# The opening normalisation of a chunk in a Mamba stage: one body earlier, its variance copied out of PSUM, its last product and x3's sum in other slots

## The chip, the cores and the metric

The kernel runs on one core of one Trainium2 chip. The metric is device time in microseconds (us). The engines are called PE (TensorE; PEld is its weight load), DVE (VectorE), ACT (ScalarE), POOL (GpSimd) and SP (SyncE, which here only issues DMAs). "Lnnn" is a line of the kernel before.

## The reference, cut to what matters

Two "metaformer" layers follow one another. The change lies in the token mixer of the second, a stack of eight Mamba layers on 4 images of 4096 tokens with 128 channels:

```python
x = x + _L1_conv_ref(_ln_c(x), ...)          # second layer's mixer
...
def _ln_c(v, eps=1e-6):
    m = jnp.mean(v, axis=1, keepdims=True)
    s = jnp.var(v, axis=1, keepdims=True)
    return (v - m) / jnp.sqrt(s + eps)
...
for l in range(DEPTH):                       # DEPTH = 8
    seq = _mamba_layer(seq, W_in[l], ...)    # conv, gates, a scan over time with 16 states per channel
    seq = _rmsnorm(seq, rms_w[l])
```

`_ln_c` is a normalisation over the 128 channels of each token: mean, difference, variance, reciprocal root, product. It stands once, ahead of the first Mamba layer. The sum `x + ...` stands once, behind the eighth.

## The kernel before, in words

Channels lie on the 128 partitions. `mamba` cuts the 4096 tokens into 8 chunks of 512. Its unit of work is a **body**: one chunk, one layer, one image. There are 8 x 8 x 4 = 256 bodies, numbered chunk x 32 + layer x 4 + image, so bodies 32k to 32k+3 are a chunk's first layer and 32k+28 to 32k+31 its eighth. Each body has 16 **slots** (j = 0 to 15). In a slot the loop at L1181 emits, in this order: two exponentials dA for the slot after next (`decay`, ACT, L973); 16 small matmuls dBx for the next slot (`inputs`, PE, L995), into one of two PSUM buffers; perhaps one step of the *previous* layer's recurrence (`rec.step`: matmul L669 on PE, tanh L672 on ACT), which runs interleaved with this stage; two scans of the slot (DVE, L1028), which need dA and dBx; behind each odd slot one product of four states with C (`times_c`, POOL, L1041 copy and L1044 product, called c0 to c7 here); then the "side" work of the slot; and 8 transposing matmuls that add up a slot's result four slots later (`add_up`, PE, L1048; in slots 0 to 3 they belong to the body before).

The side work is written out by hand in the table PLAN (L692): a row for each slot, and a bar that parts what stands ahead of `add_up` from what stands behind it. A letter names the body that a piece works for, seen from the current body o = i: n = i+1, q = i-1, m = i+2. In the kernel before, s is body i+2 and z body i+3, each only where that body belongs to layer 0. Every engine runs its instructions in the order emitted. The pieces that matter here:

- `v0`, `v1` (L846): the input projection of the next body, in PSUM banks f0 and f1, with the ACT work behind it (L849 to L855).
- `s.mean` (L808): one matmul with the averaging matrix into bank f1 (L810, two passes in the trace), the difference on DVE (L812), its square on ACT (L813). `s.var` (L815): a second matmul into bank f1 (L818) and, directly from the bank, the logarithm on ACT (L819). `s.rstd` (L1105): the exponential on ACT. `s.u` (L1109): the product on POOL. `z.fetch` (L806): the load of the next such body's input, into a single buffer.
- `q.pm`, `q.log`, `q.rstd`, `q.u` (L1098, L1102, L1105, L1109): the same kind of step for the RMS norm that ends a body.
- `q.end` (L1111): for layer 8 alone, a load of 256 KB, the sum on POOL (L1115), a store.
- `dtx1`, `turn1` (L934 on POOL, L941 on PE, L944 on ACT): the second half of the next body's scan inputs: a POOL product, four transposes into bank f1, a copy.
- `m.edge` (L822): eight small POOL instructions (L829, L835, L836).

Banks f0 and f1 are handed round among these pieces by the table BANK (L712), so that each piece waits until the reader of the one before it is done.

Bodies in which layer 0 is normalised or layer 8 is summed lie around each of the seven chunk borders. In the kernel before, s is active in bodies 30 to 33 (mod 32) and `q.end` in bodies 29 to 32. Ahead of the loop, bodies 0 and 1 are normalised in a straight line (L1157).

Of the kernel before, what the change touches and what calls it, by code (L numbers as in the profile page):

```python
# [8 lines left out]
F32 = mybir.dt.float32  # L9
AF = mybir.ActivationFunctionType  # L10
ALU = mybir.AluOpType
# [8 lines left out]
P = 128  # L20
B = 4
# [24 lines left out]
TL = 512  # L46
# [643 lines left out]


PLAN = """  # L692
n.v0 |
s.mean |
| n.tap03 n.tap02 o.C3
n.v1 | q.leave1 o.by0
n.tap01 | o.by1 q.back1
q.gate1 |
| n.tap12 q.po0 n.tap13 n.tap11
q.po1 | q.square n.pz0 n.pz1 n.silu n.silu_z0 n.silu_z1 a.exp  # L700
n.pd0 | n.pd1 n.keep
n.pt0 n.C2 n.pt1 | n.softplus0 q.pm n.softplus1 a.ln q.log q.rstd s.var s.rstd a.exp
n.dtx0 n.bt n.B |
q.u s.u | o.leave0 n.diag0
q.end n.turn0 n.skip0 n.skip1 | n.diag2
o.back0 n.diag5 | n.diag3
n.diag1 z.fetch n.C0 o.gate0 n.dtx1 m.edge | n.C1
n.diag4 n.turn1 n.diag6 |
""".strip().split("\n")
STEPS = [1, 0, 1, 2, 1, 1, 1, 0, 1, 0, 1, 0, 2, 2, 2, 1]  # L710

# [15 lines left out]
def mamba(tc, ops, I, rec, x2_d, x3_d):  # L727
# [8 lines left out]
    nc = tc.nc  # L736
# [5 lines left out]
    with ExitStack() as ctx:  # L742
# [4 lines left out]
        w = ctx.enter_context(tc.tile_pool(name="mwk", bufs=2))  # L747
        c = ctx.enter_context(tc.tile_pool(name="mc", bufs=1))
        wp = ctx.enter_context(tc.tile_pool(name="mwp", bufs=2))
        up = ctx.enter_context(tc.tile_pool(name="mu", bufs=5))  # L750
        w1 = ctx.enter_context(tc.tile_pool(name="mw1", bufs=1))
        dr = ctx.enter_context(tc.tile_pool(name="mdr", bufs=4, space=DRAM))
        psf = ctx.enter_context(tc.tile_pool(name="mpf", bufs=1, space=PSUM))
# [27 lines left out]
        us = {}  # L781
        weights = {}

        def bank(what):

            name = f"f{BANK[what]}"
            return psf.tile([P, TL], F32, tag=name, name=name)
# [10 lines left out]
        def load(l):  # L798
            given = wp.tile([P, W_GIVEN], F32, tag="given", name="given")
            nc.sync.dma_start(out=given, in_=I["m_given"][l])  # L800
            weights[l] = given


        def fetch(o):
            o.x2 = w1.tile([P, TL], F32, tag="x2", name="x2")
            nc.sync.dma_start(out=o.x2, in_=x2_d[:, o.b, o.ck * TL : (o.ck + 1) * TL])  # L806
# [8 lines left out]
        def var(o):  # L815
            o.r = w1.tile([P, TL], F32, tag="r0", name="r0")
            v = bank("var")
            nc.tensor.matmul(v, ops.avg, o.x2, start=True, stop=True)  # L818
            nc.scalar.activation(o.r, v, AF.Ln, bias=ops.eps6)  # L819


        def edge(o):  # L822

            o.edge = w.tile([P, NH, DC - 1], F32, tag="edge", name="edge")
            part = w.tile([P, NH, DC - 1, DC - 1], F32, tag="part", name="part")
            for h in range(NH):
                tl = tail[:, o.l, o.b, h, :]
                for k in range(DC - 1):
                    nc.gpsimd.tensor_tensor(  # L829
                        part[:, h, k, :],  # L830
                        tl[:, k : k + DC - 1],
                        taps[:, o.l, h, k : k + 1].to_broadcast([P, DC - 1]),
                        ALU.mult,
                    )
            nc.gpsimd.tensor_tensor(o.edge, part[:, :, 0, :], part[:, :, 1, :], ALU.add)  # L835
            nc.gpsimd.tensor_tensor(o.edge, o.edge, part[:, :, 2, :], ALU.add)  # L836
# [140 lines left out]
        def decay(o, j):  # L977
            if where(j)[0] != SP_B:
                o.dA[j] = dap.tile([P, 2, TL], F32, tag="dA", name="dA")
                exps(o, j)  # L980

        def inputs(o, j):


            sp, h = where(j)
            if sp == SP_B:
                o.dA[j] = psx.tile([P, 2, TL], F32, tag="dBx", name="dAp")
                exps(o, j)
                return
            o.dBx[j] = psx.tile([P, TL, 2], F32, tag="dBx", name="dBx")  # L990
            for n in range(NB):
                for q in range(2):
                    at = q * HQ + n * 64
                    row = slice(q * 64, (q + 1) * 64)
                    nc.tensor.matmul(  # L995
                        o.dBx[j][:, at : at + 64, :],
                        o.dtxT[h][row, n, :],
                        o.diag[row, sp, n],
                        start=True,
                        stop=True,  # L1000
                    )
# [21 lines left out]
        def scan(o, j):  # L1023
            sp, h = where(j)
            hs = states(o, j)
            for k in range(2):
                s = 2 * sp + k
                nc.vector.tensor_tensor_scan(  # L1028
                    hs[:, k, :],
                    o.dA[j][:, k, :],  # L1030
                    hs[:, k, :] if sp == SP_B else o.dBx[j][:, :, k],
                    state[:, o.l, o.b, h, s : s + 1],
                    ALU.mult,
                    ALU.add,
                )

        def times_c(o, g):
            sp, h = where(2 * g)
            f = sp // 2
            hs = o.hs[g]  # L1040
            nc.gpsimd.tensor_copy(  # L1041
                state[:, o.l, o.b, h, 4 * f : 4 * f + 4].unsqueeze(2), hs[:, :, TL - 1 : TL]
            )
            nc.gpsimd.tensor_tensor(hs, hs, o.Cb[f], ALU.mult)  # L1044
# [13 lines left out]
        def skips(o, h):  # L1058

            o.yT = psy.tile([P, NB, P], F32, tag="yT", name="yT")  # L1060
            add_turned(o, o.xD[h], start=True)

        def add_up(o, j):
            for k in range(2):
                add_turned(o, states(o, j)[:, k, :])
# [39 lines left out]
            nc.scalar.activation(o.r, o.r, AF.Exp, scale=-0.5)  # L1105

        def norm(o):
            us[o.b] = up.tile([P, TL], F32, tag="u", name="u")
            nc.gpsimd.tensor_tensor(us[o.b], o.pos, o.r, ALU.mult)  # L1109

        def end(o):  # L1111
            here = (slice(None), o.b, slice(o.ck * TL, (o.ck + 1) * TL))
            x3 = w1.tile([P, TL], F32, tag="x3", name="x3")
            nc.sync.dma_start(out=x3, in_=x2_d[here])
            nc.gpsimd.tensor_tensor(x3, x3, us[o.b], ALU.add)  # L1115
            nc.sync.dma_start(out=x3_d[here], in_=x3)


# [1 line left out]
        bodies = [Body(ck, l, b) for ck in range(NCK) for l in range(DEPTH) for b in range(B)]  # L1120

        def get(i):
            return bodies[i] if 0 <= i < len(bodies) else None

        def table(name):
# [12 lines left out]
        pieces |= {f"by{h}": lambda o, h=h: times_b(o, SP - 1 + h) for h in range(NH)}  # L1138
        pieces |= {f"C{g}": lambda o, g=g: give_c(o, g) for g in range(NS // 4)}
        pieces |= {  # L1140
            "fetch": fetch, "mean": mean, "var": var, "silu": silu_x, "keep": keep, "B": give_b,
            "bt": turn_b, "square": square, "pm": rms, "log": log, "rstd": rstd, "u": norm,
            "end": lambda o: end(o) if o.l == DEPTH - 1 else None, "edge": edge,
            "exp": table(EXP_TANH), "ln": table(EXP_LN),
        }
        plan = [[[x.split(".") for x in part.split()] for part in row.split("|")] for row in PLAN]

        def side(who, j, part):

            for k, what in plan[j][part] if part < len(plan[j]) else ():  # L1150
                if who.get(k):
                    pieces[what](who[k])

        load(0)
        for t in range(PRE):
            rec.step(t)
        for s in bodies[0:2]:  # L1157
            for what in ("fetch", "mean", "var", "rstd", "u"):
                pieces[what](s)
        fetch(bodies[2])  # L1160
        edge(bodies[0])
        for row in plan:
            for part in row:
# [7 lines left out]
        LAG = 4  # L1171
        t = PRE
        for i in range(len(bodies) + 1):
            o, n, q, s = get(i), get(i + 1), get(i - 1), get(i + 2)
            who = {"o": o, "n": n, "q": q, "m": s, "a": o or q}
            z = get(i + 3)
            who["s"] = s if s and s.l == 0 else None
            who["z"] = z if z and z.l == 0 else None
            if o and o.b == 1 and i + 3 < len(bodies):
                load((o.l + 1) % DEPTH)  # L1180
            for j in range(NSLOT):  # L1181
                if o:
                    if j + 2 < NSLOT:
                        decay(o, j + 2)
                    elif n:
                        decay(n, j + 2 - NSLOT)
                    if j + 1 < NSLOT:
                        inputs(o, j + 1)
                    elif n:
                        inputs(n, 0)  # L1190
                    if STEPS[j] > 0 and t < L:
                        rec.step(t)
                        t += 1
                    scan(o, j)
                    if j % 2:
                        times_c(o, j // 2)
                side(who, j, 0)
                if o and j in (LAG, SP + LAG):
                    skips(o, j // SP)
                if o and j >= LAG:  # L1200
                    add_up(o, j - LAG)
                elif q and j < LAG:
                    add_up(q, NSLOT - LAG + j)
                side(who, j, 1)
                if o and STEPS[j] > 1 and t < L:
                    rec.step(t)
                    t += 1
# [424 lines left out]
```

## Time and profile before

| | us |
|---|---|
| time, median of 3 runs | 15802.7 (15797.8 to 15809.1) |
| the profiled execution's own time | 15798.8 |
| its span | 15796.6 |
| first and last scan of the Mamba stage | 2209.0 and 15491.5 |

The Mamba stage is 13,282 us of the span. Distance from a body's first scan to that of the next, from the start times of L1028 in the timeline of DVE:

| body (border between chunks 1 and 2) | 61 | 62 | 63 | 64 | 65 | 66 | 67 | 68 |
|---|---|---|---|---|---|---|---|---|
| us | 50.78 | 57.66 | 58.35 | 59.05 | 60.98 | 53.54 | 50.80 | 51.51 |

Away from the borders a body takes 50.78 us, and 51.5 us where its number is divisible by 4 (a new tile of the interleaved recurrence begins there). The windows view from body 0's first scan to 3743 us and from 4034 to 5359 us has PEclk, the granted TensorE clock, at 1.00; from 3743 to 4034 us and from 5359 to 5700 us, the five bodies at a border, it is 0.96.

How to read the views: the timeline lists an engine's instructions by start, with merged length, and in brackets the idle time ahead of them and what ended it; the windows view has one row for each stretch, with busy time by engine and the granted clock. A group's row on the page has count, then busy time and mean duration, then idle time ahead of it.

### The profile page before, as it was taken

What the parts mean: (1) busy time and instruction counts of PE and PEld (TensorE: products, weight loads), DVE (VectorE), ACT (ScalarE), POOL (GpSimd) and SP (SyncE); (2) the same over time, 40 slices, a digit from 0 to 9 for tenths busy, and PEclk for the clock granted to TensorE, in tenths of its full rate; (3) what the DMA queues carried; (4) which work ended last, traced back from release to release, by engine and by line L of the source; (5) the groups of instructions that cost most, each with busy time, mean ns of one, the idle gap of its engine ahead of it and who ended that gap; (6) DMA issues with size and microseconds to landing.
All of it is one profiled execution on the core that took longest, in us unless ns stands there. A gap on an engine that the chain in (4) does not pass through costs nothing. (4 is left out here: it accounts for less than half of the span.)

```text
span 15796.6 us, 303059 instructions
## 1 busy us (share of the span) xinstructions
PE 14414.7 (91%) x120596; PEld 10829.8 (69%) x120596; DVE 13673.8 (87%) x14937; ACT 12011.2 (76%) x23557; POOL 13179.6 (83%) x9086
## 2 busy tenths in 40 slices
PE   7888779999999999999999999999999999989996
PEld 3444557777777777777777777777777777766664
DVE  8998039998999889998999899989998999989994
ACT  6887248887888778877888788878887788777773
POOL 4555039998999999998999899989999999999993
PEclk8999579999999999999999999999999999999998
DMA  0000012222222222222222222222222222222224
GB/s 22 22 22 22 15 55 98 100 104 99 101 97 99 106 96 103 98 99 100 100 104 99 99 98 99 104 99 103 98 97 102 99 104 98 99 100 95 101 99 170
DMA packets 423477, 1431.59 MB, mean 91 GB/s; under 512 B 204080, under 2 KB 204464, under 8 KB 290864
## 3 DMA queue, kind: packets, MB, share of 16 engines
q1 hardware_dynamic: 422064, 1412.21, 24.8%
q8 instruction: 953, 15.61, 0.4%
q14 instruction: 460, 3.77, 0.1%
HBM read 1353.33 MB, written 58.72 MB: 89 GB/s over the span
## 5 line engine op out<-in xcount | busy, mean ns | idle before, releaser
L1028 DVE TENSOR_TENSOR_SCAN hs<-dA,state,dBx 128x512 f32<-128x512 f32 x7168 | 8699.2, 1262 | 1039.1 <-PE dBx L995 1003.3
L1044 POOL TENSOR_TENSOR hs<-hs,Cb 128x2048 f32<-128x2048 f32 x2048 | 9294.1, 4538 | 165.5 <-POOL state L1041 0.2
L973 ACT ACTIVATE dA<-dt,A 128x512 f32<-128x512 f32 x7168 | 4734.7, 721 | 6.6 <-DVE hs L1028 0.5
L1048 PE MATMUL yT<-ident,hs 128*128 128x128 f32 x32768 | 4347.6, 277 | 7.7 <-POOL hs L1044 7.7
L1048 PEld LDWEIGHTS yT<-ident,hs 128*128 128x128 f32 x32768 | 3798.9, 145 | 770.0 <-issue 642.5
L995 PE MATMUL dBx<-diag,dtxT 64*128 64x128 f32 x57344 | 4186.6, 285 | 121.3 <-DVE hs L1028 109.3
L995 PEld LDWEIGHTS dBx<-diag,dtxT 64*128 64x128 f32 x57344 | 3513.2, 188 | 1081.5 <-issue 706.7
L672 ACT ACTIVATE z<-p 128x4 f32<-128x4 f32 x4096 | 710.0, 173 | 1844.6 <-PE p L669 1838.9
L669 PE MATMUL p<-z,vt 128*128 128x4 f32 x8192 | 1578.7, 263 | 205.4 <-ACT z L672 203.6
L669 PEld LDWEIGHTS p<-z,vt 128*128 128x128 f32 x8192 | 1350.5, 207 | 587.6 <-ACT z L672 303.1
L1016 POOL TENSOR_TENSOR hs<-Bb,dtx 128x512 f32<-128x512 f32 x1024 | 1275.8, 1283 | 0.1
L1028 DVE TENSOR_TENSOR_SCAN hs<-dAp,state,hs 128x512 f32<-128x512 f32 x1024 | 1228.2, 1261 | 0.0
L961 DVE TENSOR_TENSOR diag<-f,i 128x512 f32<-128x512 f32 x1792 | 1157.0, 670 | 7.9 <-PE f L949 7.9
L860 DVE SCALAR_TENSOR_TENSOR xc<-f,taps,xc 128x509 f32<-128x509 f32 (+2 forms) x1536 | 1129.9, 736 | 37.6 <-ACT tail L855 10.4
L1041 POOL COPY state<-hs 128x4 f32<-128x4 f32 x2048 | 391.3, 191 | 827.2 <-DVE hs L1028 825.5
L1126 ACT ACT_TABLE_LOAD x771 | 989.2, 1283 | 10.3
L278 DVE SCALAR_TENSOR_TENSOR acc<-qp,dww,acc 128x512 f32<-128x512 f32 x1184 | 886.4, 749 | 12.2
L973 ACT ACTIVATE dAp<-dt,A 128x512 f32<-128x512 f32 x1024 | 709.0, 692 | 211.8 <-DVE hs L1028 180.5
L875 PE MATMUL f<-u,given 128*128 128x512 f32 x1024 | 510.0, 620 | 329.9 <-ACT pos L1094 322.8
L849 ACT ACTIVATE xc<-f,taps 128x509 f32<-128x509 f32 x512 | 350.3, 684 | 471.2 <-PE f L846 471.2
L934 POOL TENSOR_TENSOR dtx<-dt,xc 128x512 f32<-128x512 f32 x512 | 651.6, 1273 | 12.0 <-ACT dt L928 12.0
L944 ACT COPY dtxT<-f 128x512 f32<-128x512 f32 x512 | 298.1, 582 | 443.5 <-PE f L941 443.5
(232 smaller groups left out, 16154.7 us busy)
## 6 DMA issues: line engine op xcount, KB each, us to landing
Cb<-c_d SPq DMA_DIRECT2D x1024, 1024.0 KB, 4.7
Bb<-c_d SPq DMA_DIRECT2D x256, 512.0 KB, 5.5
given<-in_m_given_dram SPq DMA_DIRECT2D x64, 640.0 KB, 5.9
slab<-in_w_dram SPq DMA_DIRECT2D x64, 512.0 KB, 9.9
x<-x_d SPq DMA_DIRECT2D x96, 256.0 KB, 4.0
x_d<-x SPq DMA_DIRECT2D x64, 256.0 KB, 2.0
c_d<-dbl SPq DMA_DIRECT2D x512, 32.0 KB, 1.6
xb<-in_x_dram SPq DMA_DIRECT2D x32, 256.0 KB, 3.2
```

What stands on the lines that cost most here:

```text
L278: nc.vector.scalar_tensor_tensor(rows(to), x, dww[:, t : t + 1], rows(o.acc), ALU.mult, ALU.add)
L669: nc.tensor.matmul(self.p[:, k, :], self.vt, self.before, start=False, stop=True, skip_group_check=True)
L672: nc.scalar.activation(self.z[:, k, :], self.p[:, k, :], AF.Tanh, scale=0.5)
L860: nc.vector.scalar_tensor_tensor(x, o.v[h][:, : TL - k], taps[:, o.l, h, DC - 1 - k : DC - k], x, ALU.mult, ALU.add)
L961: nc.vector.tensor_tensor(o.diag[:, sp], bt.unsqueeze(2).to_broadcast([P, NB, 64, 2]), i64.unsqueeze(1).unsqueeze(3).to_broadcast([P, NB, ...
L973: nc.scalar.activation(o.dA[j][:, k, :], o.dt[h], AF.Exp, scale=A[:, o.l, h, n : n + 1])
L995: nc.tensor.matmul(o.dBx[j][:, at : at + 64, :], o.dtxT[h][row, n, :], o.diag[row, sp, n], start=True, stop=True,)
L1016: nc.gpsimd.tensor_tensor(hs[:, k, :].rearrange("p (q n t) -> p q n t", n=NB, q=2), o.Bb[:, k, :].rearrange("p (q n t) -> p q n t", n=NB, ...
L1028: nc.vector.tensor_tensor_scan(hs[:, k, :], o.dA[j][:, k, :], hs[:, k, :] if sp == SP_B else o.dBx[j][:, :, k], state[:, o.l, o.b, h, s : ...
L1044: nc.gpsimd.tensor_tensor(hs, hs, o.Cb[f], ALU.mult)
L1048: nc.tensor.matmul(o.yT[:, n, :], x[:, n * P : (n + 1) * P], ops.ident, start=start and n == 0, stop=True, is_transpose=True, skip_group_c ...
L1126: return lambda o: nc.scalar.preload_act_table_set(name)
```

## The change

- s is now body i+3 and z body i+4, so the normalisation is spread over bodies 29 to 32 (mod 32), those of `q.end`. Three bodies instead of two are normalised ahead of the loop.
- `s.mean` moves from slot 1 to the head of slot 0, ahead of `n.v0`. `s.var`'s matmul moves from slot 9 to slot 1, and ACT copies its bank to SBUF at once; the logarithm (`s.lnv`) stays in slot 9 and reads SBUF.
- `s.u` moves behind the bar of slot 11, `q.end` from slot 12 to behind the bar of slot 13, `m.edge` from slot 14 (behind `n.dtx1`) to slot 15 (behind c7), `z.fetch` from slot 14 to slot 8.
- `norm` keeps its output as `o.out` too, which `end` reads, and the pool of these tiles has 6 buffers for 5.

```diff
-n.v0 |
-s.mean |
+s.mean n.v0 |
+s.var |
...
-n.pd0 | n.pd1 n.keep
-n.pt0 n.C2 n.pt1 | n.softplus0 q.pm n.softplus1 a.ln q.log q.rstd s.var s.rstd a.exp
+n.pd0 | n.pd1 z.fetch n.keep
+n.pt0 n.C2 n.pt1 | n.softplus0 q.pm n.softplus1 a.ln q.log q.rstd s.lnv s.rstd a.exp
...
-q.u s.u | o.leave0 n.diag0
-q.end n.turn0 n.skip0 n.skip1 | n.diag2
-o.back0 n.diag5 | n.diag3
-n.diag1 z.fetch n.C0 o.gate0 n.dtx1 m.edge | n.C1
-n.diag4 n.turn1 n.diag6 |
+q.u | s.u o.leave0 n.diag0
+n.turn0 n.skip0 n.skip1 | n.diag2
+o.back0 n.diag5 | q.end n.diag3
+n.diag1 n.C0 o.gate0 n.dtx1 | n.C1
+n.diag4 n.turn1 n.diag6 m.edge |
...
-        up = ctx.enter_context(tc.tile_pool(name="mu", bufs=5))
+        up = ctx.enter_context(tc.tile_pool(name="mu", bufs=6))
...
-            nc.scalar.activation(o.r, v, AF.Ln, bias=ops.eps6)
+            nc.scalar.copy(o.r, v)
+
+        def log_var(o):
+            nc.scalar.activation(o.r, o.r, AF.Ln, bias=ops.eps6)
...
-            us[o.b] = up.tile([P, TL], F32, tag="u", name="u")
-            nc.gpsimd.tensor_tensor(us[o.b], o.pos, o.r, ALU.mult)
+            o.out = us[o.b] = up.tile([P, TL], F32, tag="u", name="u")
+            nc.gpsimd.tensor_tensor(o.out, o.pos, o.r, ALU.mult)
...
-            nc.gpsimd.tensor_tensor(x3, x3, us[o.b], ALU.add)
+            nc.gpsimd.tensor_tensor(x3, x3, o.out, ALU.add)
...
-        for s in bodies[0:2]:
-            for what in ("fetch", "mean", "var", "rstd", "u"):
+        for s in bodies[0:3]:
+            for what in ("fetch", "mean", "var", "lnv", "rstd", "u"):
                 pieces[what](s)
-        fetch(bodies[2])
+        fetch(bodies[3])
...
-            o, n, q, s = get(i), get(i + 1), get(i - 1), get(i + 2)
-            who = {"o": o, "n": n, "q": q, "m": s, "a": o or q}
-            z = get(i + 3)
+            o, n, q = get(i), get(i + 1), get(i - 1)
+            who = {"o": o, "n": n, "q": q, "m": get(i + 2), "a": o or q}
+            s, z = get(i + 3), get(i + 4)
```

More of the change, by code (lines that the diff above doesn't have):

```diff
@@ L1140, in mamba @@
         pieces |= {
-            "fetch": fetch, "mean": mean, "var": var, "silu": silu_x, "keep": keep, "B": give_b,
+            "fetch": fetch, "mean": mean, "var": var, "lnv": log_var, "silu": silu_x, "keep": keep,
+            "B": give_b,
             "bt": turn_b, "square": square, "pm": rms, "log": log, "rstd": rstd, "u": norm,
```

## The prediction

> **What bounds the kernel now.** I read the page, then DVE's timeline of an ordinary body and of one at a border, then PE, the clock, ACT and POOL there.
>
> ```profile
> PE 14414.7 (91%) x120596; PEld 10829.8 (69%) x120596; DVE 13673.8 (87%) x14937; ACT 12011.2 (76%) x23557; POOL 13179.6 (83%) x9086
> ...
> L1028 DVE TENSOR_TENSOR_SCAN hs<-dA,state,dBx 128x512 f32<-128x512 f32 x7168 | 8699.2, 1262 | 1039.1 <-PE dBx L995 1003.3
> L1044 POOL TENSOR_TENSOR hs<-hs,Cb 128x2048 f32<-128x2048 f32 x2048 | 9294.1, 4538 | 165.5 <-POOL state L1041 0.2
> ```
>
> Three engines are nearly full, and what idle time the scans have ends with PE's dBx. Ordinary body 70 (first scan at 5852.54) has one large gap:
>
> ```profile
> 5886.77 2.45 DVE L1028 TENSOR_TENSOR_SCAN hs<-dA,state,dBx 128x512 f32<-128x512 f32 x2 [2.58 <-PE dBx L995]
> ...
> 5889.74 2.45 DVE L1028 TENSOR_TENSOR_SCAN hs<-dA,state,dBx 128x512 f32<-128x512 f32 x2
> ```
>
> That is slot 11; slot 12 follows without a gap. Border body 62 (first scan at 5409.87) has three:
>
> ```profile
> 5414.07 2.45 DVE L1028 TENSOR_TENSOR_SCAN hs<-dA,state,dBx 128x512 f32<-128x512 f32 x2 [1.76 <-PE dBx L995]
> 5418.29 0.69 DVE L812 TENSOR_TENSOR xm<-x,f 128x512 f32<-128x512 f32 x1 [1.77 <-PE f L810]
> ...
> 5451.02 2.45 DVE L1028 TENSOR_TENSOR_SCAN hs<-dA,state,dBx 128x512 f32<-128x512 f32 x2 [5.16 <-PE dBx L995]
> ```
>
> Its 57.66 us less 50.78 are these: 1.76 in slot 1; 1.77 ahead of the difference and about 0.6 for it; 2.58 more than usual in slot 11. The last comes from `s.var` in slot 9, which PE meets ahead of slot 11's dBx and which waits until the logarithm of q has left bank f1:
>
> ```profile
> 5448.69 1.12 PE L818 MATMUL f<-x,avg 128*128 128x512 f32 x2 [1.45 <-ACT r L1102]
> 5449.74 1.16 PE L995 MATMUL dBx<-diag,dtxT 64*128 64x128 f32 x16
> ```
>
> 1.45 + 1.12 = 2.57. The gap in slot 1 starts on POOL. Ordinarily `dtx1` ends 1.98 ahead of the next body (5901.33 against 5903.31). Two products of 1.24 each between c5 and c6 make it 0.50 late:
>
> ```profile
> 5459.55 1.30 POOL L1109 TENSOR_TENSOR u<-xm,r 128x512 f32<-128x512 f32 x1
> 5460.78 1.29 POOL L1115 TENSOR_TENSOR x<-x,u 128x512 f32<-128x512 f32 x1
> ...
> 5466.77 1.26 POOL L934 TENSOR_TENSOR dtx<-dt,xc 128x512 f32<-128x512 f32 x1
> ```
>
> PE waits for it in `turn1`, and then runs slowly:
>
> ```profile
> 5409.72 0.95 PE L941 MATMUL f<-ident,dtx 128*128 128x128 f32 x4 [2.28 <-POOL dtx L934]
> ...
> 5417.12 1.13 PE L810 MATMUL f<-x,avg 128*128 128x512 f32 x2
> ```
>
> ```profile
> 5406.52:5409.93 3.41, 1.13 (x16) 0.92 (x13) 3.41 (x5) 1.11 (x3) 3.41 (x4) 1.00 0.91 325
> 5409.93:5413.35 3.42, 3.42 (x22) 3.09 (x22) 2.38 (x3) 1.82 (x3) 3.26 (x9) 0.50 0.98 336
> ```
>
> In these rows PE's busy time comes first, the clock before the last two numbers: a 3.41 us stretch with 1.13 busy is followed by one at half clock. With the clock full, dBx for slot 1 ends 2.68 after `dtx1`; at half clock 4.28: 1.6 lost.
>
> Over the seven borders, each body's length less 50.78 (51.5 where divisible by 4; 0.1 less in the last chunk, which has no recurrence) sums to 35.4, 35.0, 30.9, 34.7, 34.6, 34.3 and 28.5: **233 us**. That is all the change can win there.
>
> [...] here windows with up to 0.49 of matmul time were followed by half clock, and those from 0.50 up almost never. [...] no such copy of the variance is in the trace yet, but copies of the same size (L1070) take 0.59 without a load.
>
> **The change, part by part** (per border body, in us).
>
> *`s.var` out of slot 9:* PE's slot 11 is ordinary again, -2.58.
>
> *Two products in slots 0 and 1.* From `turn1` to the `add_up` of slot 3 PE runs without a break: in ordinary body 71 its last ends 10.6 after the first scan, and scan 4, which needs the buffer that it frees, starts at 10.82. Body 98, whose `dtx1` was 1.27 late at full clock, lost 1.15: the cover is about 0.13. So a product here costs its length. L810 takes 0.97 (start to next start) to 1.13; I take 1.05, two make 2.10, less 0.13: **1.97**. The difference on DVE (0.6) lies inside it. Below zero it can't be, as the products exist; if the cover were complete, it would be 0. Before, only the mean stood here.
>
> *Waits of the move.* The mean waits for the copy behind `turn1` (ends 0.64 ahead of the body) and isn't held. The difference follows scan 0 at +2.36, the mean ends at about +2.0: not held. Square ends at +3.7, PE reaches the variance at +4.9: not held. On ACT the square waits for DVE with `v0`'s work and dA3 behind it; dA3 then comes at about 6.6, scan 3 at 9. The copy waits for PE (+6) with dA4 behind it, needed at 12.7. Nothing waits.
>
> *ACT in slot 9.* `s.lnv` and `s.rstd` still stand ahead of the last table load: 0.69 + 0.63 and 0.05 of gaps = 1.37 (from SBUF the logarithm may take 0.63 to 0.69). Behind them is dA for slot 12:
>
> ```profile
> 5888.93 1.34 ACT L973 ACTIVATE dA<-dt,A 128x512 f32<-128x512 f32 x2
> ```
>
> Its first half would end at 5889.65, scan 12 starts at 5889.74. With slot 11 on time again this is the next wait: 1.37 - 0.06 = **1.31**. Before, it was hidden behind the 2.58.
>
> *POOL.* From the end of slot 11's scans to the end of `dtx1` are 12.11 now; two products more make 14.59. To the next body are 14.09 + 1.31 = 15.40. So `dtx1` ends 0.81 ahead, 1.17 later than usual. The order of c6 and `q.end` makes no difference, save that the sum no longer waits for its load (0.52 in body 61). PE's idle time ahead of `turn1`: 0.5 + 1.17 less 0.06 (the exponentials come 1.37, not 1.31, later, and PE's last step waits for ACT) = 1.61, so the worst window is 1 - 1.61/3.41 = 0.53 busy: just above 0.50, full clock. Lateness **1.17**, in the body after.
>
> *Sum:* body 29: 1.97 + 1.31 = 3.28. Bodies 30, 31, 32: 1.17 more, 4.45 each, and 0.13 in 32, where the cover is used up. Body 33: 1.17 - 0.13 = 1.04. Together 17.8; seven borders 125. Saved: 233 - 125 = 108.
>
> *Start.* The third body ahead of the loop costs 8.55 (L810 at 2169.77 and 2178.32) and a copy, about 9.1. Bodies 0 to 2 lose 2.58 - 1.31, 3.55 (54.33 - 50.78) and 1.15 (51.93 - 50.78): 6.0. Net +3.1.
>
> *At nothing:* `m.edge` behind c7. c7 can start 0.4 earlier, c0 of the next body waits now 0.75 and c1 1.31; edge's 1.40 - 0.4 delays c0 by 0.3, which c1's wait takes up. Its result is needed 50 us later. If the cover were gone: 0.3 to 0.65 in every body. `z.fetch` in slot 8: SP is then waiting for `dbl`, the buffer has been free since slot 1; one issue of 0.38, and nobody behind is late. `q.end`'s store now stands ahead of C0 and C1 on SP, and goes 2.1 ahead of the body; they land 4.7 later, +3, and c0 starts at about +6. With that cover gone, c0 would be late by what exceeds it, in 28 bodies.
>
> 108 - 3 = 105. The profiled execution took 15798.8, so 15694; the median is 3.9 higher: **15698**.
>
> **The rivals.**
> 1. *Half clock stays.* 0.53 is close to 0.50. Bodies 94 and 126 had 1.84 idle and went to half; 98 had 2.08 and did not. If all four bodies after a border body do: 28 x 1.6 = 45, **15743**.
> 2. *The products are hidden.* If PE's chain isn't what holds scan 4: 28 x 1.97 = 55 less, **15643**. Against it: bodies 36 and 68 lose 0.72 to PE's added work in the same slots.
> 3. *Half clock for three windows,* as in bodies 33 and 65 (10.24 us): 28 x (1.6 + 2.6) = 118, **15816**, no change.
> 4. *Slower: `m.edge` becomes the path.* It stands between c7 and c0 in all 255 bodies. If c0's 0.75 is the only cover, 1.40 - 0.75 = 0.65 a body: 166 us, **15864**. It decides from 105/255 = 0.41 a body. Against it: c1's 1.31 behind c0, and `add_up` needs c0 only in slot 4.
>
> **How the numbers follow.** Forecast 0.57, rivals 0.25, 0.08, 0.04, 0.06. A measurement of this kernel tells 0.2% (32 us) from no change, so below 15771 it is faster: 0.90; same 0.04; slower 0.06. The range takes in the forecast with products of 0.97 to 1.13 and a few slow windows, and rival 1: 15660 to 15760; left out are rivals 2 to 4, 0.18.
>
> **What would show it.** Ordinary bodies at 50.8. Slot 11's gap 2.58 in bodies 29 to 32, and a new gap of 1.3 in slot 12 that ends with ACT's dA. Body 29 at 54, 30 and 31 at 55 (57 at half clock), 33 at 52. A gap ahead of scan 4 of some 1.2, ended by PE. PEclk near 1.00 at the borders. An ordinary body of 51.1 or more would make me wrong by rival 4, one of 58 at the borders by rival 3.

## The result, and the profile after

| | before | after |
|---|---|---|
| time, median of 9 runs | 15798.9 (15786.5 to 15809.1) | 15755.1 (15745.0 to 15763.3) |
| ratio, 95% interval | | 0.9971 (0.9962 to 0.9979) |
| the profiled execution's span | 15796.6 | 15754.2 |
| first and last scan of the Mamba stage | 2209.0, 15491.5 | 2214.8, 15448.5 |

The kernel became 0.3% faster, 44 us between the medians, where 105 were forecast. In the code after, the lines from L822 on stand 3 lower in the file: the scan is L1031, dBx L998, `times_c` L1047, the edge's last piece L839. First the page of the kernel after; a group's row ends with the idle time ahead of it and what ended that.

```profile
PE 14399.4 (91%) x120596; PEld 10805.1 (69%) x120596; DVE 13692.4 (87%) x14937; ACT 12014.9 (76%) x23591; POOL 13181.8 (84%) x9086
...
L1031 DVE TENSOR_TENSOR_SCAN hs<-dA,state,dBx 128x512 f32<-128x512 f32 x7168 | 8716.1, 1263 | 987.2 <-PE dBx L998 865.5
...
L854 ACT ACTIVATE xc<-f,edge,taps 128x1 f32<-128x1 f32 x1536 | 426.6, 350 | 450.2 <-POOL edge L839 449.9
```

Of the scans' idle time only 52 us are gone. The new thing is the last row: ACT's one-column pieces (the line serves `v0` and `v1`) wait 450 us for `m.edge`. In the kernel before the same row, among the groups of ACT, reads:

```profile
L851 ACT ACTIVATE xc<-f,edge,taps 128x1 f32<-128x1 f32 x1536 | 424.7, 351 | 2.1 <-POOL edge L836 2.1
```

By the start times of the scans in the two traces, the difference of the spans splits so (us):

| part | before | after | difference | forecast |
|---|---|---|---|---|
| up to the first scan | 2209.0 | 2214.8 | +5.8 | +9.1 |
| bodies 0 to 2 | 158.4 | 155.6 | -2.8 | -6.0 |
| bodies 29 to 34 of the seven borders | 2369.7 | 2297.9 | -71.8 | -108 |
| 133 other bodies, number not divisible by 4 | 6755.9 | 6777.5 | +21.6 | 0 |
| 48 other bodies, number divisible by 4 | 2472.4 | 2473.3 | +0.9 | 0 |
| body 220 (no recurrence), the last chunk and what follows | | | +3.9 | 0 |

So two thirds of the forecast came at the borders, and an ordinary body takes 50.95 for 50.78. Lengths of the bodies at three borders after, from the starts of L1031:

| body (mod 32) | 28 | 29 | 30 | 31 | 32 | 33 | 34 |
|---|---|---|---|---|---|---|---|
| forecast | 51.5 | 54.06 | 55.23 | 55.23 | 56.08 | 51.82 | 50.78 |
| from 60 | 51.52 | 53.68 | 57.86 | 54.86 | 56.85 | 51.81 | 50.96 |
| from 92 | 51.51 | 53.69 | 60.76 | 54.86 | 55.72 | 55.01 | 50.95 |
| from 124 | 51.52 | 53.70 | 58.11 | 58.09 | 57.07 | 51.83 | 50.96 |

Where the clock stayed full (body 29; 31 in the first two rows, 32 in the second, 33 in the other two) the forecast holds within 0.4. Three things are not in it: the 0.17 in ordinary bodies, the 58 at half clock, and body 30.

**The ordinary body.** ACT's timeline in body 70 of the kernel after (first scan at 5837.55), then POOL's and PE's; the columns are start, merged length, what ran, and in brackets the idle time ahead of it:

```profile
5840.18 0.67 ACT L852 ACTIVATE xc<-f,taps 128x509 f32<-128x509 f32 x1
5842.69 0.84 ACT L854 ACTIVATE xc<-f,edge,taps 128x1 f32<-128x1 f32 x3 [1.84 <-POOL edge L839]
...
5843.45 2.58 ACT L976 ACTIVATE dA<-dt,A 128x512 f32<-128x512 f32 x4
5845.92 0.18 ACT L672 ACTIVATE z<-p 128x4 f32<-128x4 f32 x1
```

```profile
5836.78 4.53 POOL L1047 TENSOR_TENSOR hs<-hs,Cb 128x2048 f32<-128x2048 f32 x1
5841.26 0.96 POOL L832 TENSOR_TENSOR part<-tail,taps 128x3 f32<-128x3 f32 x6
...
5842.46 0.20 POOL L839 TENSOR_TENSOR edge<-edge,part 128x6 f32<-128x6 f32 x1
```

```profile
5846.15 0.39 PE L669 MATMUL p<-z,vt 128*128 128x4 f32 x2 [0.17 <-ACT z L672]
...
5847.33 1.04 PE L1051 MATMUL yT<-ident,hs 128*128 128x128 f32 x8
```

In body 70 of the kernel before (first scan at 5852.54) the same step comes 8.36 after the first scan, for 8.60, and waits for nothing:

```profile
5860.90 0.39 PE L669 MATMUL p<-z,vt 128*128 128x4 f32 x2
```

Read it from the end. PE waits 0.17 for a tanh of the recurrence; the `add_up` behind that step comes 0.17 late. The tanh is late because ACT stood 1.84 at L854 and did its four exponentials only then. And ACT stood because the eight pieces of `m.edge` run behind c7, which ends only 3.8 after the first scan, so the edge is done at +5.1.

**The half clock.** Body 125 to 126 in the kernel after: PE's wait ahead of `turn1`, and what follows; then the windows view there, aligned with the windows of the clock (PE's busy time first, the clock before the last two numbers).

```profile
8725.32 0.66 PE L944 MATMUL f<-ident,dtx 128*128 128x128 f32 x4 [1.67 <-POOL dtx L937]
...
8729.46 2.06 PE L810 MATMUL f<-x,avg 128*128 128x512 f32 x2
8731.31 1.91 PE L849 MATMUL f<-u,given 128*128 128x512 f32 x2
```

```profile
8723.07:8726.48 3.41, 1.74 (x19) 1.53 (x16) 3.41 (x5) 1.25 (x3) 3.33 (x4) 1.00 0.49 163
8726.48:8729.90 3.42, 3.42 (x23) 2.86 (x22) 2.05 (x2) 1.52 (x4) 3.42 (x1) 0.50 1.01 400
8729.90:8733.31 3.41, 3.41 (x6) 1.24 (x6) 1.70 (x2) 0.63 (x2) 1.38 (x9) 0.50 1.10 369
```

1.74 / 3.41 = 0.51 busy, and the next two windows run at half clock, though PE is busy all through them. In them stand the mean (2.06 for the 1.10 of body 62, at full clock) and the input projection.

**Body 30.** SP's queue, ACT and PE in body 62 of the kernel after (first scan at 5411.47):

```profile
5409.44 0.32 SPq L1119 DMA_DIRECT2D x_d<-x  x1
5409.81 0.93 SPq L916 DMA_DIRECT2D Cb<-c_d  x2
5410.78 0.53 SPq L650 DMA_DIRECT2D wx<-wx_d  x1
```

```profile
5419.17 0.60 ACT L653 ACTIVATE wx<-wx,sh,sc 128x256 f32<-128x256 f32 x1 [5.34 <-DMA wx<-wx_d]
5419.68 0.61 ACT L813 ACTIVATE x<-xm 128x512 f32<-128x512 f32 x1
```

```profile
5420.35 1.12 PE L818 MATMUL f<-x,avg 128*128 128x512 f32 x2 [2.93 <-ACT x L813]
```

wx is the input of the interleaved recurrence's next tile. That tile begins in body 32 (mod 32), but its load and ACT's scaling of it (L653) stand in body 30. The load is issued behind the store of x3 and two 1 MB loads of C, and ACT has it 8.39 after its issue. ACT waits 5.34 for it, with the square for the variance behind, which begins 4.31 after DVE ended its difference (L812, at 5415.37); and PE waits 2.93 for that square, with dBx behind. At the six borders with the recurrence ACT waits 2.6 to 5.5 for wx in body 30; in the kernel before it waited at one of them, 0.78.

### The profile page after: what moved, and what is told of

It reads as the page before. It is cut to its first block, busy times and chain, and to the rows that moved or that the text cites. A ratio compares the mean times of both kernels' runs of the same rounds, so it can differ in the third digit from the quotient of the medians.

```text
span 15754.2 us, 303022 instructions
## 1 busy us (share of the span) xinstructions
PE 14399.4 (91%) x120596; PEld 10805.1 (69%) x120596; DVE 13692.4 (87%) x14937; ACT 12014.9 (76%) x23591; POOL 13181.8 (84%) x9086
## 5 line engine op out<-in xcount | busy, mean ns | idle before, releaser
L1031 DVE TENSOR_TENSOR_SCAN hs<-dA,state,dBx 128x512 f32<-128x512 f32 x7168 | 8716.1, 1263 | 987.2 <-PE dBx L998 865.5
L1047 POOL TENSOR_TENSOR hs<-hs,Cb 128x2048 f32<-128x2048 f32 x2048 | 9296.0, 4539 | 166.2 <-POOL state L1044 1.3
L998 PE MATMUL dBx<-diag,dtxT 64*128 64x128 f32 x57344 | 4187.2, 285 | 72.7 <-DVE hs L1031 46.9
L998 PEld LDWEIGHTS dBx<-diag,dtxT 64*128 64x128 f32 x57344 | 3511.2, 188 | 1027.3 <-issue 697.6
L1031 DVE TENSOR_TENSOR_SCAN hs<-dAp,state,hs 128x512 f32<-128x512 f32 x1024 | 1228.6, 1262 | 0.0
L854 ACT ACTIVATE xc<-f,edge,taps 128x1 f32<-128x1 f32 x1536 | 426.6, 350 | 450.2 <-POOL edge L839 449.9
```

The costliest lines, as they stand in the source:

```text
L998: nc.tensor.matmul(o.dBx[j][:, at : at + 64, :], o.dtxT[h][row, n, :], o.diag[row, sp, n], start=True, stop=True,)
L1031: nc.vector.tensor_tensor_scan(hs[:, k, :], o.dA[j][:, k, :], hs[:, k, :] if sp == SP_B else o.dBx[j][:, :, k], state[:, o.l, o.b, h, s : ...
```

## The experiments

Each is measured beside runs of the kernel before on the same chip, whose medians were 15800.9 (E1, E2, E4, E5) and 15804.5 (the others). The first four take the three causes singly.

### E1: the edge back where it was

```diff
-n.diag1 n.C0 o.gate0 n.dtx1 | n.C1
-n.diag4 n.turn1 n.diag6 m.edge |
+n.diag1 n.C0 o.gate0 n.dtx1 m.edge | n.C1
+n.diag4 n.turn1 n.diag6 |
```

> The changed kernel with m.edge back in slot 14 behind dtx1; all else as changed. Theory (edge): the three one-column pieces of ACT (L854) wait for the edge in slot 0 of the very next body, hold ACT 1.84, and so the recurrence's step on PE: ordinary bodies return from 50.95 to 50.78, 133 of them save about 22, the total falls by 20 to 28 to about 15730. Border bodies keep their half clock (57 to 58). Rival (the 0.17 comes from other work of the change, such as the SP queue): ordinary bodies stay at 50.95, the total at 15755.

Measured: 15728.3 (15725.4 to 15732.3), ratio 0.9954 (0.9939 to 0.9969). The 133 ordinary bodies sum to 6755.4, 50.78 each, as before the change. From the groups of ACT:

```profile
L854 ACT ACTIVATE xc<-f,edge,taps 128x1 f32<-128x1 f32 x1536 | 424.5, 351 | 2.1 <-POOL edge L839 2.1
```

### E2: the edge alone, in the kernel before

```diff
-n.diag1 z.fetch n.C0 o.gate0 n.dtx1 m.edge | n.C1
-n.diag4 n.turn1 n.diag6 |
+n.diag1 z.fetch n.C0 o.gate0 n.dtx1 | n.C1
+n.diag4 n.turn1 n.diag6 m.edge |
```

> The kernel before with m.edge alone moved to slot 15. Theory (edge): ordinary bodies go from 50.78 to 50.95, ACT has a gap of about 1.8 ahead of L851, the total rises by 20 to 35 to about 15825. Rival: no change in ordinary bodies, 15799.

Measured: 15829.8 (15823.4 to 15837.8), ratio 1.0018 (1.0011 to 1.0025): the one part of the change that loses, by itself. An ordinary body takes 50.93; those 133 lose 18.9, the borders 7.0, the last chunk 3.7. The wait is there in the groups of ACT:

```profile
L851 ACT ACTIVATE xc<-f,edge,taps 128x1 f32<-128x1 f32 x1536 | 426.5, 350 | 444.2 <-POOL edge L836 444.2
```

### E4: PE kept busy ahead of turn1

Ten more transposes, whose result nobody reads, stand ahead of `turn1` in slot 15 of bodies 29 to 32 (mod 32); the edge stays in slot 15 too. It adds work to PE.

```diff
+            if h == 1 and o.filler:
+                for k in range(10):
+                    nc.tensor.transpose(p[:, 0:P], o.dtx[:, 0, 0:P], ops.ident)
...
+            if n:
+                n.filler = bool(who["s"])
```

> The changed kernel with ten transposes more, of data that nobody reads, ahead of turn1 in the bodies whose layer-0 work is active, so that PE has about 1.1 of work in its idle 1.65. Nothing else differs. Theory (half clock): no window there falls below half busy, PEclk stays at 1.00 at the borders, bodies 31 and 32 (mod 32) that took 57 to 58 take 54.9 and 55.6, bodies 30 stay at 57.8 where they wait for wx; the total falls by 15 to 40. Rival (the length of 58 comes from the work itself, not from the clock): they stay at 58, and the total is the same or higher by what the ten transposes cost.

Measured: 15719.9 (15718.6 to 15724.3), ratio 0.9949 (0.9934 to 0.9964). Half-clock time falls from 71.7 to 3.4 us in the first six borders and from 20.5 to 1.5 in the seventh, the sum of the seven from 2297.9 to 2265.1. Bodies 31 now take 54.84 to 54.87 at six of the seven borders (the seventh is the last chunk's, without recurrence), bodies 33 take 51.8. From 126 to 127, PE's timeline and the window that holds the wait:

```profile
8768.82 1.29 PE L946 MATMUL f<-ident,dtx 128*128 128x128 f32 x10
8770.62 0.66 PE L948 MATMUL f<-ident,dtx 128*128 128x128 f32 x4 [0.51 <-POOL dtx L938]
```

```profile
8769.36:8772.77 3.41, 2.90 (x31) 2.50 (x31) 3.41 (x5) 1.46 (x3) 3.33 (x3) 1.00 0.77 274
```

`turn1` starts as late as without them, 1.65 after PE's last step of the recurrence for 1.66, since the product on POOL is as late; the clock differs, 1.00 in the window that follows for 0.50. More work on PE makes the kernel 35 us faster. Bodies 30 still take 56.6 to 57.8 at five borders without any half-clock window, so what they lose beyond 54.86 there isn't the clock; the sixth takes 59.3 with the one window that is left. In this trace ACT waits 4.03 to 5.28 for wx in those five bodies, and each is longer than 54.86 by its wait less 2.3.

### E5: x3's store behind C0 and C1

The sum stays in slot 13; its store moves behind the bar of slot 15.

```diff
-n.diag4 n.turn1 n.diag6 m.edge |
+n.diag4 n.turn1 n.diag6 m.edge | q.put
...
-            nc.sync.dma_start(out=x3_d[here], in_=x3)
+            o.x3 = x3
+
+        def put(o):
+            here = (slice(None), o.b, slice(o.ck * TL, (o.ck + 1) * TL))
+            nc.sync.dma_start(out=x3_d[here], in_=o.x3)
```

> The changed kernel with x3's store taken out of end and issued behind the bar of slot 15, so that on SP the loads of C0 and C1 no longer stand behind a store that waits for the sum. Theory (queue): wx, the recurrence's next tile, no longer lands right behind 2 MB of C at +7.7 but some 3 to 4 earlier; ACT no longer waits 5.3 for it in bodies 30 (mod 32), which fall from 57.9 to about 54.9 at full clock (from 58.1 at half clock little); the total falls by 5 to 20. Rival (the store is no obstacle, wx is late by its own issue): body 30 stays as it is, total 15755.

Measured: 15741.6 (15727.7 to 15747.4), ratio 0.996 (0.9946 to 0.9975). Body 30 takes 54.85 or 54.86 at four of six borders, and 58.10 and 56.40 at the two where a half-clock window falls into it. SP's queue and ACT at body 94 (first scan at 7065.29):

```profile
7062.04 0.32 SPq L916 DMA_DIRECT2D Cb<-c_d  x1
7063.27 0.32 SPq L1123 DMA_DIRECT2D x_d<-x  x1
7063.63 0.53 SPq L650 DMA_DIRECT2D wx<-wx_d  x1
```

```profile
7068.48 0.60 ACT L653 ACTIVATE wx<-wx,sh,sc 128x256 f32<-128x256 f32 x1 [0.82 <-DMA wx<-wx_d]
```

ACT now has the same load 4.85 after its issue (8.39 in body 62 of the kernel after), and waits 0.82 for it. The body's 60.76 became 54.85. Whether wx stood behind the 2 MB of C or shared the bandwidth with them, these two times don't tell.

### E3 and E6: an early edge, and c0 held up without one

E1 leaves a rival: behind c7 the edge also delays c0 on POOL. E3 puts it into slot 2, ahead of C3 and between c0 and c1, where POOL waits anyway. E6 is E3 and puts eight POOL instructions like the edge's, into a tile that nobody reads, behind c7: it adds work to POOL, and c0 is as late as after the change.

```diff
-| n.tap03 n.tap02 o.C3
+| n.tap03 n.tap02 m.edge o.C3
...
-n.diag4 n.turn1 n.diag6 m.edge |
+n.diag4 n.turn1 n.diag6 m.idle |
```

(In E3 the last row is without `m.idle`.)

> The changed kernel with m.edge in slot 2, behind c0 and ahead of c1, where POOL waits 1.1 to 1.3 for the scans anyway. Theory (edge): the result is there 48 us ahead of its use, ordinary bodies take 50.78, the total falls by 20 to 28 as with m.edge in slot 14, to about 15730. Border bodies as in the changed kernel, with their half clock where the windows fall so.

> m.edge in slot 2, and in slot 15, behind c7, the same eight POOL instructions once more with a result that nobody reads. POOL thus starts c0 as late as in the changed kernel. Theory (edge): the delay comes from ACT's wait for the edge, so ordinary bodies stay at 50.78. Rival (POOL: c0 starts later, and what follows on POOL is late): ordinary bodies take 50.95, 22 us or more in all.

Measured: E3 15730.7 (15727.4 to 15734.9), ratio 0.9954 (0.9939 to 0.9969); E6 15729.7 (15726.9 to 15742.9), ratio 0.9956 (0.9939 to 0.9972). The ordinary bodies take 50.78 in E3 and 50.79 in E6. POOL and ACT in body 70 of E6 (first scan at 5831.82; its lines are 14 lower than those of the kernel after):

```profile
5835.54 0.95 POOL L846 TENSOR_TENSOR part<-tail,taps 128x3 f32<-128x3 f32 x6
...
5836.86 0.19 POOL L1058 COPY state<-hs 128x4 f32<-128x4 f32 x1
```

```profile
5834.60 0.66 ACT L866 ACTIVATE xc<-f,taps 128x509 f32<-128x509 f32 x1
5835.17 0.83 ACT L868 ACTIVATE xc<-f,edge,taps 128x1 f32<-128x1 f32 x3
```

c0 begins 5.04 after the first scan here and 5.05 in the kernel after (5842.60); ACT doesn't wait, and the body is as short as before. So it is the wait for the result, not the place on POOL. The forecast's cover for c0 (1.31 of wait in front of c1) was right.

### E7: all of POOL's new work behind dtx1

E3, and `q.end`'s sum and `s.u` behind `dtx1` in slot 14, the store in slot 15 as in E5. `dtx1` is then no later than in an ordinary body.

```diff
-q.u | s.u o.leave0 n.diag0
+q.u | o.leave0 n.diag0
...
-o.back0 n.diag5 | q.end n.diag3
-n.diag1 n.C0 o.gate0 n.dtx1 | n.C1
-n.diag4 n.turn1 n.diag6 |
+o.back0 n.diag5 | n.diag3
+n.diag1 n.C0 o.gate0 n.dtx1 q.end s.u | n.C1
+n.diag4 n.turn1 n.diag6 | q.put
```

> m.edge in slot 2, x3's sum and s.u behind dtx1 in slot 14, x3's store in slot 15. dtx1 is no longer late, PE's idle time ahead of turn1 is at most the ordinary 0.5. Theory: no half clock at the borders without any filler, no 1.17 of lateness: bodies 29 to 32 take 53.7 each (54.5 where divisible by 4), body 33 takes 50.8; border sums (bodies 29 to 34) fall from about 328 to about 317, 77 in all, and the ordinary bodies give 22: the total is 15650 to 15670. Rival (the two products then push c7 and what hangs on it): bodies 30 to 33 stay above 54.8.

Measured: 15658.1 (15652.2 to 15663.2), ratio 0.9908 (0.9893 to 0.9922). No window of the first six borders is at half clock (6.8 us in the seventh); the sum of the seven is 2220.9. Bodies 29 to 32 take 53.7, 53.6 to 54.8, 53.6 and 54.5. The wait in slot 12 is left, here in body 62:

```profile
5428.49 2.45 DVE L1031 TENSOR_TENSOR_SCAN hs<-dA,state,dBx 128x512 f32<-128x512 f32 x2 [1.22 <-ACT dA L976]
```

### E8: the exponential of the normalisation later

E7, with `s.rstd` away from slot 9, where dA for slot 12 stands behind it.

```diff
-n.pt0 n.C2 n.pt1 | n.softplus0 q.pm n.softplus1 a.ln q.log q.rstd s.lnv s.rstd a.exp
+n.pt0 n.C2 n.pt1 | n.softplus0 q.pm n.softplus1 a.ln q.log q.rstd s.lnv a.exp
...
-o.back0 n.diag5 | n.diag3
+o.back0 n.diag5 s.rstd | n.diag3
```

> The kernel of the run before with s.rstd taken from ahead of the table load in slot 9 to slot 13, where ACT waits for PE anyway. Theory: the gap ahead of slot 12's scans shrinks by the exponential's 0.65, from 1.22 to about 0.6, in 28 bodies: 18 less, 15632 to 15652. Rival (another wait comes in its place, such as ACT's table load for the exponential): no change against the run before.

Measured: 15644.5 (15637.4 to 15649.5), ratio 0.9899 (0.9884 to 0.9914), the fastest of all. The borders' sum is 2200.6. DVE, PE and POOL at body 62 (first scan at 5388.71):

```profile
5428.63 2.45 DVE L1031 TENSOR_TENSOR_SCAN hs<-dA,state,dBx 128x512 f32<-128x512 f32 x2 [0.56 <-ACT dA L976]
```

```profile
5440.19 0.66 PE L944 MATMUL f<-ident,dtx 128*128 128x128 f32 x4 [0.43 <-POOL dtx L937]
```

```profile
5438.86 1.28 POOL L937 TENSOR_TENSOR dtx<-dt,xc 128x512 f32<-128x512 f32 x1
5440.09 1.28 POOL L1118 TENSOR_TENSOR x<-x,u 128x512 f32<-128x512 f32 x1
5441.31 1.28 POOL L1112 TENSOR_TENSOR u<-xm,r 128x512 f32<-128x512 f32 x1
```

Slot 12 waits 0.66 less, about one exponential of 0.64 on ACT; `turn1` waits 0.43 for 1.67.

## Why the prediction was right or wrong

**Right.** `s.var` out of slot 9 gave back its 2.58: slot 11 waits as in an ordinary body, and the copy brought the new wait in slot 12 (body 62 of the kernel after):

```profile
5451.50 2.45 DVE L1031 TENSOR_TENSOR_SCAN hs<-dA,state,dBx 128x512 f32<-128x512 f32 x2 [2.58 <-PE dBx L998]
...
5455.76 2.45 DVE L1031 TENSOR_TENSOR_SCAN hs<-dA,state,dBx 128x512 f32<-128x512 f32 x2 [1.22 <-ACT dA L976]
```

The copy takes 0.59 (L819, 32 of them), and no table load stands at its line; L1129 has 771, as many as L1126 before. From slot 11's scan to slot 12's are 4.26, for 2.97 in ordinary body 70 of before: 1.29 more, forecast 1.31. `dtx1` ends 0.80 to 0.85 ahead of the body (0.81), and PE's idle time ahead of `turn1` is 1.65 to 1.69 (1.61) at the six borders with the recurrence. Two products cost less than the 1.97: in body 61 scan 4 waits

```profile
5370.20 2.45 DVE L1031 TENSOR_TENSOR_SCAN hs<-dA,state,dBx 128x512 f32<-128x512 f32 x2 [0.92 <-PE p L669]
```

and with the difference on DVE (0.65) that is about 1.6. Body 29 shows it too: 53.69 for 54.06. Over 28 bodies that is some 10 us more saved than forecast.

**Right by luck.** Prelude and first bodies make +3.0 together, for +3.1, but the parts are +5.8 for +9.1 and -2.8 for -6.0, so two misses cancel. And the first scan's time moves by 5 between traces with the same prelude (2209.0 before, 2203.6 in E2).

Of the 105 forecast, 61 are missing. What failed are three terms that the forecast put at nothing: the edge, the clock and the store.

**Wrong, 1: "At nothing: `m.edge` behind c7. ... Its result is needed 50 us later."** Piece m works for body i+2, but the pieces of body i+2 that read the edge are `v0` and `v1`, which run in slots 0 and following of body i+1: the very next slots. I followed the move on the engine that executes it and checked who stands behind it there; I didn't look for the reader of its result, ACT's L854, and where that stands. What it showed instead is a wait of ACT and then of PE that costs 0.17 in 133 bodies, 22.5 us by the table (21.6 + 0.9, the bodies divisible by 4 hardly losing). Rival 4 had the edge as the path, but by c0 on POOL, which E6 excludes. E1 takes it back (-27), E2 has it alone (+29).

**Wrong, 2: "0.53 busy: just above 0.50, full clock."** The idle time was right to 0.1, but it made windows of 0.51 to 0.52. The windows of 0.50 to 0.52 of before (borders and last chunk), of which 1 in 17 was followed by half clock, lay nearly all (16) behind body 220, where there is no recurrence. After, 12 of 17 such windows in the first six borders were followed by half clock, and none of 16 behind body 220. So the limit was read from windows unlike those that mattered. Over bodies 20 to 219 of all ten traces, full-clock windows that were busy for 0.51 or 0.52 (rounded) were followed by half clock in 59 of 79 cases (13 of 18 in the traces of before and after), those of 0.53 to 0.55 in none of 13 (one of 0.56 was). An estimate from these 13: a window of 0.53 as forecast would have kept the clock. The term failed because its idle time was 0.06 short and because it took full clock for granted above 0.50, where 12 of these 17 windows were followed by half clock.

The price per body differs as well, and not because the mean stands in it. In the traces of the kernel after, E1, E3, E5 and E6, a body 31 (mod 32) takes 1.5 to 1.6 more than at full clock where one window is at half clock, as forecast, and 3.2 more (58.1 for 54.86) where it is two in a row. Bodies 33, which have no mean, show the same 1.5 to 1.6 and 3.2; bodies 32, where they had half clock, had one window, at 1.1 to 1.7. In bodies 31 and 33 of these five traces it was one window where the half clock began up to 0.20 after the body's first scan, and two where it began from 0.22 on; why the second stays at half clock, with PE busy all through the first (3.42 of 3.42 from 8726.48 in the kernel after), is open. Of the 14 half-clock bodies of the first six borders seven have two. Rival 1 had the half clock, at 45 us for 28 bodies with one window each; E4 puts it at 33 in the borders and 35 in the medians.

**Wrong, 3: "`q.end`'s store now stands ahead of C0 and C1 on SP ... c0 starts at about +6."** C0's landing was followed, and c0 isn't what suffers. But what SP issues later is held as well, and in body 30 that is wx: in body 62 it goes out 1.34 after the store and 0.69 ahead of the body, and ACT has it 8.39 later. E5 shows it: with the store out of the way, body 94 goes from 60.76 to 54.85. By E4's bodies 30 it costs 1.7 to 3.0 at five borders and 4.4 at the sixth, where a half-clock window follows PE's wait: 15.3 together.

The sum at the borders: 71.8 + 33 for the clock + 15 for wx = 120, less the 10 by which the products were cheaper = 110, against 108 forecast. With 22.5 for the edge, the 59 that were missing at the borders and in ordinary bodies are named within a few us; the clock's and wx's shares come from one trace, E4's. The 3.9 at the end is not named: the last chunk is 4.1 longer in E1, with the edge back, and what lies behind the borders is 3.7 longer in E2, with the edge alone. Of the 3.9, 2.7 lie in the last body, which has 11.5 us of half clock for 6.8. What decides whether a window of 0.51 or 0.52 is followed by half clock stays open: busy time, as the trace models it, doesn't tell them apart.

## What to carry to other kernels

Where a step moves in a hand-written order, follow two threads: what it delays on its own engine, and when its result is first read; a letter that says "for the body after next" isn't a due time. Behind a store that waits, follow every load that SP issues later, not only the first: here it was the third, wx, that ACT waited for, 2.6 to 5.5. A limit such as the forecast's 0.50 should be read from windows that resemble those which the change makes (1 in 17 was followed by half clock before, 12 of 17 after), and a forecast that lies 0.03 from it needs both cases in its sum. Late side work (E7) or work that fills the gap (E4) took the question away here: half clock in the first six borders fell from 71.7 us to none and to 3.4.

## What the runs showed of the hardware

In bodies 20 to 219 of the ten traces, a full-clock window of 3.41 us in which PE was busy for 0.51 or 0.52 was followed by half clock in 59 of 79 cases, one of 0.53 to 0.55 in none of 13. In the traces of five kernels (after, E1, E3, E5, E6) one window at half clock cost bodies 31 and 33 1.5 to 1.6 us, two in a row 3.2, with and without the mean. Ten unread transposes ahead of a wait, 1.29 us of work, raised a window of 0.51 to 0.85 (2.90 of 3.41) and saved 35 us over the kernel: more work on PE, less time. And a load of 128 KB that ACT had 4.85 after its issue in E5 (body 94), where one load of 1 MB went out 1.59 ahead of it, took 8.39 in the kernel after (body 62), where two had been issued within a microsecond ahead of it.
